# An attention kernel's setup in another order: Wk's transposes, sums and loads, Wq's spreading, and one batch's first head sums

## The chip, the cores and the metric

The kernel runs on one core of a Trainium2 chip. The metric is the device time of one execution in microseconds (us). A core has the engines PE (TensorE, matrix products; its weight loads are shown apart as PEld), DVE (VectorE), ACT (ScalarE), POOL (GpSimd) and SP (SyncE, which issues most of the DMAs). Each works through a list of instructions of its own, in order, and they wait for each other by semaphores.

## The reference

There are 16 batches with 100 query rows of width 640, and for each batch 722 context rows of width 384, of which the last 4 are "ca" tokens. There are 8 heads of 80 columns. Everything is in float32.

```python
query = hidden_states @ Wq
keyt, valt = enc @ Wk, enc @ Wv              # enc: the first 718 context rows
hs = _mha(query, keyt, valt)
ca_q1 = jnp.einsum('btc,th->bch', ca, Wq_ca)[:, indices, :]   # 100 picked columns
ca_hs1 = _mha(ca_q1, residual, residual)
ca_q2 = ca_hs1 @ Wq
ca_hs2 = _mha(ca_q2, ca @ Wk_ca, ca @ Wv_ca)
out = (hs + ca_hs2) @ Wout + b_out + residual
```

`_mha` is plain attention with a softmax over the keys of each head. `hs` is the large part, `ca_hs2` a small one with 4 keys.

## The kernel before, in words

**Stages.** A setup loads the weights and makes what the batches share; then a loop over 16 batches runs, in which scores, softmax, keys and values of the next batch, and the output projection are interleaved. Products of matrices are made by a scheme with fewer products and more sums (15 "forms" of sums of blocks), so the weights and the encoder rows are first added up: `weight_sums` (L546) for Wv, Wk and Wk's last part, `enc_sums` (L516) on POOL for each batch's encoder rows. A form's product goes to one of five banks of PSUM (A to E), and is copied (ACT, L423) or added (DVE, L421) into `kT` or `vs`.

**The setup around the change**, in the order of the text:

- SP's loads (from L287): encoder rows of batch 0, the ca tokens, Wk_ca, Wq transposed (L310), more encoder rows, x of batches 0 and 1 (`xT`, L313), `ca` of batch 0 (L315), then Wk transposed by `load_packed` (L317), Wq in five chunks of 128 rows (L323), Wv_ca (L324). Wk goes to the place of `kT`, Wq to the place of `sts`. `load_packed` turns the 640 rows (8 heads of 80) into five chunks of 128 rows: chunk c in 0 to 3 holds the first 64 rows of heads c and c + 4, chunk 4 the last 16 rows of all eight heads.
- PE makes values of batch 0 (L391), then `k_ps` (L1367) and the five m products (L1391); DVE copies each to `m_sb` (L1399), SP stores each to `m_d` (L1403).
- `y` (L970, in `Second.products`) multiplies x with `m2`, which POOL masks (`keys`, L941). DVE takes a part of y as `g` (`take`, L983), ACT copies the rest (L987).
- Wk's five chunks are transposed on PE (`w_ps`, L1415, chunk 4 first) and copied by ACT (L1418) to `wk4` and `wk_sb`.
- Wq's five chunks are spread by DVE into the order of heads that the products need, three copies each (L1426, L1432).
- DVE makes the 12 sums of Wk's blocks (L546), then takes the last head of `g` (L983). With that POOL makes the first scores of batch 0 (`scores1`, L999 and L1006), then 12 small sums of `wk4`.
- PE makes the last chunk of batch 0's keys (`last_keys`, `kT_ps`, L702), the keys by forms (`k_psA` and so on, L481), `va` (L1457) between them, and then the queries (`q_ps`, L560).
- SP loads the encoder rows of batch 1 (L234), its `ca` (L960) and the next `xT` (L218). `ca` has one buffer, so its load waits until POOL has read the one before.

**What sets the order.** In the setup the tile framework's scheduler decides: it orders each engine's instructions by its own model and by the order of the text, except where `in_order`/`keep_in_program_order` holds an instruction in its place, or `tc.issue_after(x)` puts the block behind x. From `tc.manual_schedule` on, the loop over the batches is in the order of the text.

**DMA issue.** The loads of SP and ACT use eight semaphores in turn, so a load is issued only when the eighth load before it has landed.

**Batch 14** (b = 14, `B - 2`): after its products with the values (`a_ps`, L1799), `read(g)` takes the reciprocal of the sums (L1747) and for each of four heads multiplies and adds `hs2` in one DVE instruction (L1759). In this batch `read(0)` stands in the middle of the second half, next to the search for the largest score of batch 15 (L891 to L926 and L918 on ACT), whose subtraction (L1025) and exponential (L1033) follow. The transposition of `hs` (L1197) and the output sums (`xn`, L1152 on POOL, L1339 on DVE) come later.

Of the kernel before, what the change touches and what calls it, by code (L numbers as in the profile page):

```python
# [10 lines left out]
ALU = mybir.AluOpType  # L11
# [3 lines left out]
B, S, H = 16, 100, 640  # L15
NH, D = 8, 80
CAD, T = 384, 4
SK = 722 - T
P = 128
HC = H // P  # L20
# [8 lines left out]
ROWS = NH * S  # L29
# [26 lines left out]
for h in range(NH):  # L56
    lo = h * D
    while lo < (h + 1) * D:
        c = lo // P
# [8 lines left out]
RG = 4  # L68
# [5 lines left out]
def load_packed(load, to, w):  # L74

    rows = w.rearrange("(h k) n -> h k n", h=NH)
    for h in range(NH):
        r, c = divmod(h, RG)
        load(out=to[64 * r : 64 * r + 64, c], in_=rows[h, :64])
    load(out=to[:, 4], in_=rows[:, 64:])  # L80


# [60 lines left out]
def kernel(  # L143
# [18 lines left out]
    nc = tc.nc  # L162
# [35 lines left out]
    def wide(name):  # L198
        return main.tile([P, ROWS], F32, tag="wide", name=name, bufs=2)

    sts = [main.tile([P, 2, ROWS], F32, name=f"st_{i}") for i in range(NP)]
# [58 lines left out]
    def in_order(dma):  # L260
        tc.keep_in_program_order(dma)
# [5 lines left out]
    wk_sb = const.tile([P, NF, 2, P], F32, name="wk_sb")  # L267
# [12 lines left out]
    enc = enc_tile("enc_0"), rest_tile("rest_0")  # L280
# [13 lines left out]
    for g in range(2):  # L294
        for c in range(CC):
            nc.scalar.dma_start(
                out=wv_sb[:, 2 * c + g],
                in_=wv[c * P : (c + 1) * P, g * (H // 2) : (g + 1) * (H // 2)],
# [13 lines left out]
    xT = inp.tile([P, 2, HC, S], F32, tag="xT", name="xT_0")  # L312
    in_order(nc.sync.dma_start(out=xT, in_=xt[0:2].rearrange("b p c s -> p b c s")))  # L313
    ca_0 = small.tile([S, T, S], F32, tag="ca", name="ca_0")
# [26 lines left out]
    for h, c, r, s, k in PIECES:  # L341
        nc.gpsimd.dma_start(
            out=m2[s : s + k, c, h - HEADS[c][0], :T],
# [153 lines left out]
    def enc_sums(enc):  # L497

        at = lambda f: a_form(enc, f)
        raw = lambda u, c: a_raw(enc, u - 1, c - 1)  # L500
        for out, left, right, op in (
            (at(7), raw(2, 3), raw(3, 1), ALU.add),
            (at(11), raw(3, 2), raw(3, 3), ALU.add),
            (at(8), at(11), raw(2, 3), ALU.subtract),
            (at(10), raw(1, 3), at(11), ALU.subtract),
            (at(9), raw(2, 1), raw(2, 2), ALU.add),
            (at(2), raw(1, 1), at(9), ALU.subtract),
            (at(9), at(9), raw(3, 1), ALU.subtract),
            (at(5), raw(1, 1), raw(2, 1), ALU.subtract),
            (at(5), at(5), raw(2, 3), ALU.add),  # L510
            (at(11), raw(1, 3), raw(3, 3), ALU.subtract),
            (at(11), at(11), raw(3, 1), ALU.add),
            (at(4), at(2), at(10), ALU.add),
            (at(4), at(4), raw(1, 2), ALU.add),
        ):
            nc.gpsimd.tensor_tensor(out, left, right, op)  # L516
# [7 lines left out]
    def weight_sums(engine, w, late=None, there={}):  # L524


        at = lambda f: there.get(f, w[:, W_AT[f]])
        raw = lambda c, g: w[:, 2 * (c - 1) + g - 1]
        if w is wk4:
            at, raw = w4_form, w4  # L530
        for f, left, right in (
            (0, raw(1, 2), raw(1, 1)),
            (11, raw(2, 2), raw(3, 2)),
            (12, raw(3, 2), raw(3, 1)),
            (5, raw(2, 2), raw(1, 2)),
            (7, raw(3, 2), at(5)),
            (13, raw(3, 1), at(7)),
            (1, raw(2, 1), raw(3, 1)),
            (3, raw(1, 1), at(7)),
            (6, raw(2, 1), raw(1, 1)),  # L540
            (10, raw(3, 1), raw(2, 2)),
            (2, raw(1, 1), raw(2, 2)),
            (14, raw(2, 1), raw(2, 2)),
        ):
            if late is None or late == (f in (5, 7, 13, 3, 14)):
                made = engine.tensor_tensor(at(f), left, right, ALU.subtract)  # L546
        return made
# [380 lines left out]
    def load_m(b):  # L928
        if b < 2:
            return lambda c: m_sb[c][:, b * HT : (b + 1) * HT]  # L930
        mb = small.tile([P, HC, HT], F32, tag="mb", name=f"mb_{b}", bufs=2)
        nc.sync.dma_start(
            out=mb, in_=m_d[:, :, b * HT : (b + 1) * HT].rearrange("c p n -> p c n")
        )
        return lambda c: mb[:, c]

    def keys(m):

        for c, heads in enumerate(HEADS):
            n = len(heads)  # L940
            made = nc.gpsimd.tensor_tensor(  # L941
                m2[:, c, :n, T:],
                m(c).unsqueeze(1).to_broadcast([P, n, HT]),
                hmask[:, c, :n].unsqueeze(2).to_broadcast([P, n, HT]),
                ALU.mult,
            )
        return made

    class Second:
# [35 lines left out]
        def copy(self):  # L985
            self.y = y_sbs[self.b % 2]
            nc.scalar.copy(self.y[:, :, :HT], self.y_v[:, :, T:])  # L987
            if self.b > 1:
                self.take(0, NH)
# [66 lines left out]
        def load(self, engine=nc.sync, behind=None):  # L1056
            self.vb = [self.piece(engine, t, behind) for t in range(2)]
# [318 lines left out]
    for n, heads in enumerate(HEADS):  # L1376
        cols = len(heads) * B * T
# [10 lines left out]
    for c in range(HC):  # L1388
# [12 lines left out]
            m_ps.rearrange("p (h b t) -> p h b t", h=NH, b=B),  # L1401
        )
        nc.sync.dma_start(out=m_d[c], in_=m_sb[c])  # L1403
    second = Second(0, xT, ca_0)
    enc_sums(enc)
    masked = keys(load_m(0))
    second.products()
    summed = second.take(0, NH - 1)
    second.copy()

    order = (HC - 1, *range(HC - 1))
    for c in order:
        w_ps = psum(f"w_ps_{c}")
        for cc in range(CC):
            nc.tensor.transpose(  # L1415
                w_ps[:, cc * P : (cc + 1) * P], wkt_sb[:, c, cc * P : (cc + 1) * P], ident
            )
        act(  # L1418
            wk_sb[:, c % 2 : 6 : 2, c // 2] if c < HC - 1 else wk4,
            w_ps[:, : CC * P].rearrange("p (a n) -> p a n", a=CC),  # L1420
        )

    with tc.issue_after(summed.ins):
        for c in range(HC):
            for r in range(2):
                nc.vector.tensor_copy(  # L1426
                    wq_sb[:, c, : 4 * P].rearrange("p (n r k) -> p n r k", n=RG, r=2)[
                        :, :, r
                    ],
                    wq_in[c].rearrange("p (r n k) -> p r n k", r=2, n=RG)[:, r, :, :64],  # L1430
                )
            moved = nc.vector.tensor_copy(  # L1432
                wq_sb[:, c, 4 * P :].rearrange("p (h k) -> p h k", h=NH),
                wq_in[c].rearrange("p (h k) -> p h k", h=NH)[:, :, 64:],
            )
    with tc.issue_after(moved.ins):
        made = weight_sums(nc.vector, wk_sb)
    with tc.issue_after(made.ins):
        second.take(NH - 1, NH)
    made = second.scores1()  # L1440
    with tc.issue_after(made.ins):
        weight_sums(nc.gpsimd, wk4)
        nc.scalar.copy(
            sts[0].rearrange("p a r -> p (a r)")[96:],
            low[96:].to_broadcast([P - 96, 2 * ROWS]),
        )
    with tc.issue_after(masked.ins):
        keys(load_m(1))
    last_keys(0, enc)
    first_keys = Keys(0, enc)  # L1450
    first_keys.go(8)
    va = wide("va")[:, : H // 2]
    va_ps = bank("va_ps")
    turn[0] += 1
    for c in range(CC):
        for n in range(2):
            nc.tensor.matmul(  # L1457
                va_ps[n * B * T : (n + 1) * B * T, : H // 2],
                cat_sb[:, c, :],
                wvca_sb[:, c, n * (H // 2) : (n + 1) * (H // 2)],  # L1460
                start=(c == 0),
                stop=(c == CC - 1),
            )
    nc.scalar.copy(va, va_ps[:, : H // 2])
    va_d = dram.tile([B * T, H], F32, name="va_d")
    for n in range(2):
# [2 lines left out]
            in_=va[n * B * T : (n + 1) * B * T],  # L1469
        )  # L1470
    first_keys.go(NF)
    with tc.issue_after(first_keys.added.ins):
        second.softmax1()

# [18 lines left out]
    for b in range(B):  # L1493
# [249 lines left out]
        def read(g):  # L1743

            a_v = a_vs[g]
            rs = small.tile([S, 4], F32, tag="rs", name=f"rs_{b}_{g}")
            nc.vector.reciprocal(rs.unsqueeze(2), a_v[:, :, D : D + 1])  # L1747
            cols = slice(4 * g * D, 4 * (g + 1) * D)
            if b == 0:
                nc.vector.tensor_tensor(  # L1750
                    hs[:S, cols].rearrange("p (h d) -> p h d", h=4),
                    a_v[:, :, :D],
                    rs.unsqueeze(2).to_broadcast([S, 4, D]),
                    ALU.mult,
                )
                return
            for h in range(4):
                part = slice((4 * g + h) * D, (4 * g + h + 1) * D)
                nc.vector.scalar_tensor_tensor(  # L1759
                    hs[:S, part],  # L1760
                    a_v[:, h, :D],
                    rs[:, h : h + 1],
                    hs2[:, part],
                    ALU.mult,
                    ALU.add,
                )

        if b in MIXED:
            steps = (0, 6), (0, 18), (1, 6)
# [112 lines left out]
```

## Time and profile before

| what | us |
|---|---|
| median of three runs (lowest, highest) | 907.91 (907.47, 909.91) |
| the profiled execution, as the device timed it | 908.96 |
| its span in the trace | 907.2 |
| PE busy | 900.4 |
| DVE, POOL, ACT busy | 719.7, 705.8, 460.1 |
| setup until the first query product | 50.0 |

The profile shows one execution. A row of the timeline gives the start and the length in us, the engine, the line of the kernel, the operation, the tiles and the count, and in brackets how long the engine stood idle before and what ended that. Rows of equal work that follow each other are merged, so a row's length spans them all. In a row of waits stand the total, the count and the longest. In a row of stretches (from:to) stand the length, the busy time of PE, PEld, DVE, ACT and POOL with their counts, the granted clock of PE (1.00 throughout), the busy share of the 16 DMA engines, and GB/s. The chain of waits follows the end of the run back, step by step, to what released each step.

### The profile page before, as it was taken

The numbers are of one execution on the slowest core, as the hardware profiler recorded it, in microseconds if no ns is written. First come the engines' busy times: TensorE is split into PE (matmuls) and PEld (weight loads), VectorE is DVE, ScalarE is ACT, GpSimd is POOL, SyncE is SP. The second block draws the span as 40 slices with busy tenths as digits, with TensorE's granted clock in tenths as the row PEclk, the third lists the DMA queues.
The fourth block names the chain that finished last, engine by engine and source line by source line (L and its number), as shares of the span: only waits on it lengthen the run. The fifth ranks groups of instructions, "written<-read, shape, count | busy, mean of one in ns | idle before, by whom it ended". The sixth has DMA issues, their size and how long they took to land.

```text
span 907.2 us, 28486 instructions
## 1 busy us (share of the span) xinstructions
PE 900.4 (99%) x12200; PEld 747.1 (82%) x12200; DVE 719.7 (79%) x1285; ACT 460.1 (51%) x906; POOL 705.8 (78%) x683
## 2 busy tenths in 40 slices
PE   9999999999999999999999999999999999999998
PEld 6798889787797878878798787988879788797866
DVE  3569796989849898796987969888984899849983
ACT  2345543747437573644737446374742747436441
POOL 7687999797868879696896959958797688967623
PEclk9999999999999999999999999999999999999999
DMA  8731103031301312130121301103130031300211
GB/s 265 262 120 57 48 14 87 24 107 53 112 4 44 88 33 74 54 105 32 48 60 54 106 33 53 56 25 106 54 83 32 24 107 53 98 32 25 60 44 40
DMA packets 50730, 62.99 MB, mean 69 GB/s; under 512 B 13698, under 2 KB 37954, under 8 KB 50604
## 3 DMA queue, kind: packets, MB, share of 16 engines
q1 hardware_dynamic: 48956, 59.18, 21.4%
q8 instruction: 96, 1.57, 0.7%
q10 hardware_dynamic: 1024, 1.15, 0.4%
q0 software_dynamic: 624, 0.85, 0.3%
q14 instruction: 30, 0.25, 0.1%
HBM read 55.59 MB, written 5.57 MB: 67 GB/s over the span
## 4 chain that ended last, share of the span: by engine, by line
PE 92%; DVE 4%; DMA 2%; SPq 1%; issue 0%; ACTq 0%; DVEq 0%
PE a_ps L1799 12%; PE s_ps L800 11%; PE v_psA L450 10%; PE k_psA L481 9%; PE v_psB L450 8%; PE k_psB L481 7%; PE o_ps L1278 5%; PE k_psA L761 4%; PE v_psC L450 3%; PE k_psC L481 3%; PE q_ps L618 2%; PE q_ps L560 2%; PE v_psD L450 2%; PE v_psE L450 2%; PE q_psA L618 1%; DMA xT<-in_xt 1%
## 5 line engine op out<-in xcount | busy, mean ns | idle before, releaser
L999 POOL TENSOR_TENSOR e<-ca,g 100x800 f32<-100x800 f32 x64 | 100.7, 1584 | 98.6 <-ACT kT L423 78.7
L1799 PEld LDWEIGHTS a_ps<-vs,st 120*64 120x64 f32 (+3 forms) x3072 | 119.0, 124 | 10.1 <-issue 0.7
L1799 PE MATMUL a_ps<-vs,st 120*64 120x81 f32 (+3 forms) x3072 | 122.8, 233 | 0.0
L516 POOL TENSOR_TENSOR enc<-enc 128x240 f32<-128x240 f32 x144 | 109.1, 768 | 11.3 <-DMA enc<-in_enct 4.2
L1515 DVE TENSOR_TENSOR st<-st,over 120x1600 f32<-120x1600 f32 x48 | 115.1, 2400 | 0.0
L450 PE MATMUL v_psA<-wv_sb,enc 128*120 128x320 f32 x352 | 109.3, 433 | 0.0
L1110 POOL TENSOR_TENSOR hs<-vb,p 100x640 f32<-100x640 f32 x64 | 93.1, 1466 | 9.6 <-issue 4.8
L1117 POOL TENSOR_TENSOR hs<-hs,hs 100x640 f32<-100x640 f32 x48 | 93.2, 1942 | 3.8
L481 PE MATMUL k_psA<-enc,wk_sb 128*128 128x240 f32 x384 | 95.4, 371 | 0.6 <-DVE wk_sb L546 0.6
L1006 POOL TENSOR_TENSOR e<-e,e 100x800 f32<-100x800 f32 x48 | 91.9, 1914 | 3.8
L450 PE MATMUL v_psB<-wv_sb,enc 128*120 128x320 f32 x296 | 91.9, 433 | 0.0
L1523 ACT ACTIVATE st<-st 120x1600 f32<-120x1600 f32 x48 | 73.9, 1539 | 25.1 <-DVE st L1515 24.7
L481 PEld LDWEIGHTS k_psA<-enc,wk_sb 128*128 128x128 f32 x384 | 71.4, 190 | 17.1 <-DVE wk_sb L546 1.0
L450 PEld LDWEIGHTS v_psA<-wv_sb,enc 128*120 128x120 f32 x352 | 64.2, 183 | 25.0 <-DVE vs L421 0.5
L1527 DVE TENSOR_TENSOR most<-most,st 120x800 f32<-120x800 f32 x64 | 67.0, 1047 | 13.8 <-ACT st L850 12.3
L481 PE MATMUL k_psB<-enc,wk_sb 128*128 128x240 f32 x320 | 77.9, 366 | 0.0
L800 PE MATMUL s_ps<-qp,kT 64*56 64x100 f32 (+1 forms) x3072 | 73.7, 248 | 0.3 <-issue 0.3
L800 PEld LDWEIGHTS s_ps<-qp,kT 64*56 64x56 f32 (+1 forms) x3072 | 67.2, 130 | 5.9 <-issue 4.6
L450 PEld LDWEIGHTS v_psB<-wv_sb,enc 128*120 128x120 f32 x296 | 54.1, 183 | 21.9 <-DVE vs L421 0.4
L856 ACT COPY st<-s_ps 120x800 f32<-120x800 f32 x64 | 49.8, 830 | 39.6 <-PE s_ps L800 39.4
L1185 ACT COPY hsT<-turned_hs 32x160 f32<-32x160 f32 (+7 forms) x244 | 67.7, 278 | 3.0
L481 PEld LDWEIGHTS k_psB<-enc,wk_sb 128*128 128x128 f32 x320 | 60.7, 190 | 8.1
(209 smaller groups left out, 1898.3 us busy)
## 6 DMA issues: line engine op xcount, KB each, us to landing
vb<-va_d SPq DMA_DIRECT2D x62, 250.0 KB
enc<-in_enct SPq DMA_DIRECT2D x30, 240.0 KB
enc<-in_enct SPq DMA_DIRECT2D x15, 360.0 KB
xT<-in_xt SPq DMA_DIRECT2D x8, 500.0 KB
rest<-in_enct SPq DMA_DIRECT2D x31, 120.0 KB
xn<-in_x SPq DMA_DIRECT2D x11, 320.0 KB
out<-xn SPq DMA_DIRECT2D x11, 320.0 KB
ca<-in_cas SPq DMA_DIRECT2D x16, 156.2 KB
```

Of the source, the lines that this page charges most:

```text
L450: nc.tensor.matmul(at[0][j][:KN, : H // 2], a_form(self.enc, f)[:, j * KN : (j + 1) * KN], wv_there.get(f, wv_sb[:, W_AT[f]]), start=first ...
L481: nc.tensor.matmul(at[:, i * KT : (i + 1) * KT], wk_sb[:, W_AT[f], i], a_form(self.enc, f), start=(first and i == 0), stop=last, skip_grou ...
L516: nc.gpsimd.tensor_tensor(out, left, right, op)
L800: nc.tensor.matmul(s_ps[at][k0:k1, cols], w, rhs, start=not begun & {(at, k) for k in range(k0, k1, 32)}, stop=last, skip_group_check=True,)
L999: first = nc.gpsimd.tensor_tensor(to, self.ca[:, t, :].unsqueeze(1).to_broadcast([S, NH, S]), g[:, :, t].unsqueeze(2).to_broadcast([S, NH, ...
L1006: made = nc.gpsimd.tensor_tensor(e, e, to, ALU.add)
L1110: first = nc.gpsimd.tensor_tensor(to, self.vb[t][:S].rearrange("p (h d) -> p h d", h=NH), p2[:, :, t].unsqueeze(2).to_broadcast([S, NH, D] ...
L1117: nc.gpsimd.tensor_tensor(sums, sums, to, ALU.add)
L1185: nc.scalar.copy(self.hsT(r)[32 * m : 32 * m + 32, :, first - lo : end - lo], turned[32 * i : 32 * i + 32, :, m, first - at : end - at],)
L1515: return nc.vector.tensor_tensor(st[i], st[i], top.over[:KN].unsqueeze(1).to_broadcast([KN, 2, ROWS]), ALU.subtract,)
L1523: nc.scalar.activation(st[i], st[i], AF.Exp, scale=SCALE)
L1799: nc.tensor.matmul(a_v[lo:hi, h % 4], st[i // 2][: KEYS[i], i % 2, h * S + lo : h * S + hi], block(i, h // 4)[: KEYS[i], h % 4], start=(i ...
```

## The change

1. Wk is loaded by five DMAs instead of nine: chunks 0 to 3 in one DMA each, over both heads (source: 2 blocks of 64 rows), chunk 4 as before (8 blocks of 16 rows).
2. The transposes of Wk and their copies stand ahead of `Second` in the text, and Wk's sums on DVE right behind them; PE then makes all 15 transposes before y.
3. Wq's spreading comes behind Wk's sums, chunks 0 to 2 on DVE, chunks 3 and 4 on ACT behind the first eight key forms.
4. The fill of `sts[0]`'s spare rows on ACT moves behind the keys; the first va product is held in its place.
5. In batch 14 the first half's four head sums become four products on ACT and one sum of 320 columns on POOL.

Built, the instructions stand so: PE has, after the m products, 15 transposes, y, `kT_ps`, and then the keys in the order A, B, D (D, A, B before). DVE has the 12 sums directly behind the m copies and `qmask`, then the first take of g, nine spreading copies, the second take. ACT has six spreading copies between the first three key copies and va's copy, and the fill behind the last key copy of batch 0. SP has batch 1's `ca` and the next `xT` ahead of batch 1's three encoder loads, which stood in front of them. POOL has the new sum ahead of the `xn` sums. From batch 0's scores to batch 14 nothing is changed on any engine.

```diff
 def load_packed(load, to, w):
     rows = w.rearrange("(h k) n -> h k n", h=NH)
-    for h in range(NH):
-        r, c = divmod(h, RG)
-        load(out=to[64 * r : 64 * r + 64, c], in_=rows[h, :64])
+    for c in range(RG):
+        load(out=to[:, c], in_=rows[c::RG, :64])
     load(out=to[:, 4], in_=rows[:, 64:])
...
-    second = Second(0, xT, ca_0)
-    enc_sums(enc)
-    masked = keys(load_m(0))
-    second.products()
-    summed = second.take(0, NH - 1)
-    second.copy()
-
     order = (HC - 1, *range(HC - 1))
     for c in order:
         w_ps = psum(f"w_ps_{c}")
...
-    with tc.issue_after(summed.ins):
-        for c in range(HC):
+    made = weight_sums(nc.vector, wk_sb)
+    second = Second(0, xT, ca_0)
+    enc_sums(enc)
+    masked = keys(load_m(0))
+    second.products()
+    second.take(0, NH - 1)
+    second.copy()
+
+    def spread_wq(copy, chunks):
+
+        for c in chunks:
             for r in range(2):
-                nc.vector.tensor_copy(
+                copy(
...
-            moved = nc.vector.tensor_copy(
+            moved = copy(
...
+        return moved
+
+    with tc.issue_after(made.ins):
+        moved = spread_wq(dve, range(3))
     with tc.issue_after(moved.ins):
-        made = weight_sums(nc.vector, wk_sb)
-    with tc.issue_after(made.ins):
         second.take(NH - 1, NH)
     made = second.scores1()
     with tc.issue_after(made.ins):
         weight_sums(nc.gpsimd, wk4)
-        nc.scalar.copy(
-            sts[0].rearrange("p a r -> p (a r)")[96:],
-            low[96:].to_broadcast([P - 96, 2 * ROWS]),
-        )
...
     first_keys.go(8)
+    spread_wq(lambda *ends: tc.keep_in_program_order(act(*ends)), range(3, HC))
...
-            nc.tensor.matmul(
+            made = nc.tensor.matmul(
                 va_ps[n * B * T : (n + 1) * B * T, : H // 2],
...
+            if c == n == 0:
+                in_order(made)
...
     first_keys.go(NF)
+    in_order(
+        nc.scalar.copy(
+            sts[0].rearrange("p a r -> p (a r)")[96:],
+            low[96:].to_broadcast([P - 96, 2 * ROWS]),
+        )
+    )
...
+                if b == B - 2 and g == 0:
+                    nc.scalar.mul(hs[:S, part], a_v[:, h, :D], rs[:, h : h + 1])
+                    continue
                 nc.vector.scalar_tensor_tensor(
...
+            if b == B - 2 and g == 0:
+                nc.gpsimd.tensor_tensor(hs[:S, cols], hs[:S, cols], hs2[:, cols], ALU.add)
```

## The prediction

> **What bounds the kernel now.** I read the page first, then the waits of PE (TensorE) by its weight loads (PEld), then the timeline and the chain of waits over the first 100 us, where all but one edit lies.
>
> ```profile
> span 907.2 us, 28486 instructions
> PE 900.4 (99%) x12200; PEld 747.1 (82%) x12200; DVE 719.7 (79%) x1285; ACT 460.1 (51%) x906; POOL 705.8 (78%) x683
> PE 92%; DVE 4%; DMA 2%; SPq 1%; issue 0%; ACTq 0%; DVEq 0%
> ```
>
> PE is busy for 99% of the span and is 92% of the chain that ended last. What other engines save is worth nothing, except where PE waits for it; and a new wait of PE comes off nothing else, it is added to the end. So I look for PE's waits, old and new.
>
> ```profile
> PEld w_ps L1415 <- DVE qmask L1476: 0.8, 1, 0.8
> PEld k_psA L481 <- DVE wk_sb L546: 1.0, 1, 1.0
> PEld w_ps L1415 <- ACT wk_sb L1418: 0.3, 1, 0.3
> ```
>
> These are the setup's waits in the whole run: about 2.1 us of weight-load time, before Wk's transposes and before the first key product. More the setup can't return. Now the stretch itself; the last two rows are from the chain.
>
> ```profile
> 27.31 0.83 PE L970 MATMUL y_ps<-m,xT 128*64 128x72 f32 x16
> 28.76 0.52 PE L1415 MATMUL w_ps<-ident,kT 128*128 128x128 f32 x3 [0.62 <-DMA kT<-in_wkt]
> 29.48 0.97 PEld L1415 LDWEIGHTS w_ps<-ident,kT 128*128 128x128 f32 x9
> 30.41 0.30 PEld L702 LDWEIGHTS kT_ps<-enc,wk 128*128 128x128 f32 x2
> ...
> 36.28 1.08 PE k_psA L481 x4
> ...
> 50.03 8.46 PE q_ps L560 x50
> 85.73 3.65 PE kT_ps L702 x18
> 96.29 0.75 PE y_ps L970 x20
> ```
>
> From the end of the m products (27.31) to the first query product (50.03) go 22.72 us. Pure work in it: 15 transposes at 0.103 (nine from 29.48 to 30.41) are 1.55; y 0.75; kT_ps 3.65; keys with va 13.75, plus 0.81 for the pair of D in front of them, less 0.27 (the first piece took 1.08 where others take 0.81): 14.29. With 0.15 for y, which has to wait for the third copy of a transpose, 20.4 us.
>
> **The new order.** After the m products PE does all 15 transposes, then y, then kT_ps, then the keys. If Wk is there at 27.31, q_ps begins at 27.31 + 20.4 = 47.7, 2.3 us earlier. In the old order y's first 16 products filled part of the wait for Wk; now y stands behind the transposes on PE, and the first transposes are those of chunk 4, whose load is issued last. So all hangs on when the fifth load lands.
>
> **Wk in five loads.** In bytes it is the same. But a load is not always spread over all 16 DMA engines, as these rows show (DMA share and GB/s are the last columns; in the SP rows L317 is Wk, L1062 va).
>
> ```profile
> 13.00:16.00 3.00, 3.00 (x13) 2.05 (x12) 0.00 (x0) 0.85 (x2) 2.77 (x6) 1.00 1.03 410
> 18.00:20.00 2.00, 2.00 (x38) 1.67 (x35) 0.91 (x4) 0.00 (x0) 0.00 (x0) 1.00 1.03 315
> 20.00:21.00 1.00, 1.00 (x6) 0.75 (x5) 0.31 (x2) 0.18 (x1) 0.98 (x2) 1.00 0.69 132
> 26.10:26.90 0.80, 0.80 (x8) 0.80 (x7) 0.69 (x1) 0.00 (x0) 0.78 (x4) 1.00 0.66 164
> 167.20:168.00 0.80, 0.80 (x5) 0.54 (x4) 0.74 (x4) 0.00 (x0) 0.72 (x2) 1.00 0.66 262
> ...
> 19.90 1.74 SPq L317 DMA_DIRECT2D kT<-in_wkt  x3
> ...
> 23.70 1.32 SPq L317 DMA_DIRECT2D kT<-in_wkt  x2
> ...
> 164.64 0.71 SPq L1062 DMA_DIRECT2D vb<-va_d  x2
> ```
>
> Loads of 128 rows fill all 16: share 1.03, 410 GB/s, 25.6 GB/s an engine. At 167.2 two loads of 100 rows are under way together, and still only 0.66 of the engines work, at 262 GB/s: ten engines (16 would give 410), and the same ten for both, or the two would have covered more. At 26.1 the old ninth Wk load runs nearly alone; its source is 8 blocks of 16 rows, and the rate is 164 GB/s, under half. Sixteen for 128, ten for 100, half or fewer for 8 blocks: the engines go by the count of the outermost dimension, and loads that get fewer share the same ones. The new loads `rows[c::RG, :64]` have 2 blocks of 64 rows: I take two engines, the same two for the four loads. [...]
>
> One of the four loads is 192 KB (196,608 bytes), 98,304 bytes for each of the two engines: 3.84 us at 25.6 GB/s; 4.80 at 164 / 8 = 20.5 GB/s, the rate of the ninth load with its start in it. I take 4.2, nearer to the dense rows. The queue ahead (share 1.03 up to 20, 0.69 after) is through at about 20.5; the first three loads are issued by then and the rest follow at once, so nothing but the two engines paces them. 20.5 + 4 x 4.2 = 37.3. The fifth load (8 blocks) has 24,576 bytes on each of eight engines, behind the others on the two: 1.05, so 38.35, and PE begins its transposes at 38.45, 11.1 us after the m products. 38.45 + 20.4 = 58.85 for q_ps, against 50.03: **+8.8 us**. Bounds: drained at 20 and 3.84 a load gives 36.4, so +6.8; drained at 21 and 4.80 gives 41.5, so +11.9.
>
> **What else moves**, at that time:
>
> ```profile
> 29.71 0.48 DVE L1426 COPY wq_sb<-st 128x256 f32<-128x256 f32 x2
> 30.09 1.27 ACT L1418 COPY wk_sb<-w_ps 128x384 f32<-128x384 f32 x3
> 33.46 4.11 DVE L546 TENSOR_TENSOR wk_sb<-wk_sb 128x256 f32<-128x256 f32 x12
> 37.71 3.04 POOL L999 TENSOR_TENSOR e<-ca,g 100x800 f32<-100x800 f32 x2 [6.70 <-DVE g L983]
> ...
> 44.13 0.43 ACT L1464 COPY va<-va_ps 128x320 f32<-128x320 f32 x1 [5.37 <-PE va_ps L1457]
> ...
> 47.93 0.32 SPq L960 DMA_DIRECT2D ca<-in_cas  x1
> ...
> 53.16 0.69 POOL L516 TENSOR_TENSOR enc<-enc 128x240 f32<-128x240 f32 x1
> 56.13 1.30 DVE L1025 TENSOR_TENSOR e<-e,over 100x800 f32<-100x800 f32 x1
> 60.92 2.14 POOL L516 TENSOR_TENSOR enc<-enc 128x240 f32<-128x240 f32 x3
> 62.37 0.88 ACT L1033 ACTIVATE e<-e 100x800 f32<-100x800 f32 x1
> ...
> 66.86 1.08 PE L481 MATMUL k_psA<-enc,wk_sb 128*128 128x240 f32 x4
> ```
>
> - Wk's sums: ScalarE's five copies of the transposes end near 41.2 (0.42 each), the sums 12 x 0.343 later at 45.2; the first eight, after which k_psA went before, at 43.9. PE comes to k_psA at 44.55. Hidden, with 0.6 to spare.
> - Wq's chunks 0 to 2 on DVE (0.48 for two of the three copies, about 0.7 in all), then the last head of g: POOL's score products start at 47.5 instead of 37.71, 9.8 later against PE's 8.8. What they lead to was ready at 57.43 (L1025) for an exponential at 62.37; the 1.0 is hidden.
> - Chunks 3 and 4 on ScalarE: no row has such a copy; between half and all of the 0.42 that 384 columns take, 6 of them 1.3 to 2.5, in ScalarE's idle 5.37 before va. Nothing. The 1.5 us fill of st, now ahead of the queries' copies, ends long before the first scores.
> - Wq, wvca and the m stores queue behind Wk on the two engines, at 0.8 us per Wq load and 2.5 for wvca: 42.5 and 45. The sums hold DVE until 45.2, and va comes 6 us into the keys, at 51. Hidden.
> - On SP the loads of batch 1's enc now stand behind its ca, which waits for POOL's last score product (47.93 before, 57.7 now). They land near 63, POOL's 9.9 us of sums (53.16 to 63.06) end near 73; they ended at 63.06 before a product at 66.86, which is now at 75.7. Hidden, with 2.5 us.
>
> **Batch 14.**
>
> ```profile
> 849.80 3.30 POOL L1152 TENSOR_TENSOR xn<-xn,bias 128x640 f32<-128x640 f32 x3
> 855.68 0.93 DVE L1759 SCALAR_TENSOR_TENSOR hs_sb<-a_ps,rs,hs 100x80 f32<-100x80 f32 x4
> 857.19 1.73 ACT L918 COPY spread<-mx 64x800 f32<-64x800 f32 x2 [0.83 <-DVE mx L905]
> 860.00 0.99 DVE L1025 TENSOR_TENSOR e<-e,over 100x800 f32<-100x800 f32 x1
> 861.19 1.68 ACT L850 COPY st<-s_ps 120x400 f32<-120x400 f32 x4 [0.31 <-PE s_ps L800]
> 862.74 1.00 ACT L1033 ACTIVATE e<-e 100x400 f32<-100x400 f32 x2
> 871.71 0.49 DVE L1339 TENSOR_TENSOR xn<-o_ps,xn 128x320 f32<-128x320 f32 x1 [0.27 <-issue]
> ```
>
> DVE loses 0.93 us, ScalarE gains four products ahead of the spread, whose price no row has: from DVE's own 0.23 each to twice that. The spread moves by between 0 and +0.9. The subtraction that follows ended at 860.99; its exponential came at 862.74, behind the copies of L850, so 1.7 us are covered, and an earlier subtraction wins nothing. POOL's added sum, after the products, holds the xn sums (four, some 5 us) till about 858; they end at 863 and are needed at 871.71. Zero, both ways.
>
> **The sum.** The profiled execution took 908.96 for a span of 907.2. By this its changed twin has 917.8; on the median of 907.91 the forecast is 916.7 us, with the bounds 914.7 and 919.8.
>
> **Rivals.**
> 1. The new loads use all 16 engines. Wk then lands about 25.5, before 27.31, and q_ps moves to 47.7: 907.91 - 2.3 = 905.6, not slower. For it: 128 destination rows, and 410 GB/s for such loads. Against: the ninth load has 128 destination rows too and ran at 164. It decides at 27.31 + 2.3 = 29.6: Wk landing before that is a gain, later a loss. Chance 0.09.
> 2. Two engines each, but another pair for each load. Four loads side by side end at 21 + 4.2, and it is 905.6 again. Against: the two vb loads kept to one set of ten. Chance 0.05.
> 3. Two engines, and each slower than 20.5 GB/s, for rows that come from memory one at a time: half the rate, 10.2, would put Wk at 61 and the time near 940. Against: 26 GB/s an engine in the vb row, also with fewer than 16. Chance 0.03.
>
> **Chances.** Forecast 0.83. The range 914.0 to 920.0 holds it nearly whole, and leaves out the rest, 0.17. A difference under 0.3% (2.7 us) is about what a measurement of this kernel can't tell from none; rivals 1 and 2 (2.3) lie in it. Slower by over 0.3%: 0.86; within: 0.13; faster, which would need more than all of the setup's waits: 0.01.
>
> **What would show it.** Right: PE idle for some 11 us before w_ps, ended by the DMA of kT; a DMA share near 0.13 (2 of 16) and some 50 GB/s between 28 and 36; the waits for Wk's sums gone from PE's list; nothing new from batch 0's scores on. Wrong: transposes at 27.3 with no wait. If the wait is there but far from 11 us, the rate of one engine was wrong; if a second wait of PE follows it, one of the covers above.

## The result, and the profile after

The changed kernel takes **923.33 us** (median of 6 runs, 922.43 to 924.76) against 907.86 for the kernel before (6 runs beside it, 907.47 to 909.91): ratio 1.0168, 95% interval 1.0155 to 1.0181, 15.5 us slower. The forecast was 916.7, with a range of 914.0 to 920.0. The sign and the mechanism were right; the size, 8.8 us, was little more than half of what came. The profiled execution took 923.1 us for a span of 921.4, which is 14.2 more than the span of before; the kernel before was profiled in an execution 1.1 us above its median of 907.86.

The head of the page, as it was read of before:

```profile
span 921.4 us, 28485 instructions
PE 902.8 (98%) x12200; PEld 749.5 (81%) x12200; DVE 723.1 (78%) x1275; ACT 462.8 (50%) x916; POOL 709.5 (77%) x684
PEclk9799999999999999999999999999999999999999
PE 93%; DMA 3%; DVE 2%; SPq 1%; ACT 0%; issue 0%; ACTq 0%; DVEq 0%
```

PE is the bound as before. New is a 7 in the row of the granted TensorE clock, in the second slice of 23 us. In the chain the DMA's share rose from 2% to 3% and DVE's fell from 4% to 2%. The waits of PE, and one of its weight loads:

```profile
PE w_ps L1407 <- DMA kT<-in_wkt: 12.2, 1, 12.2
PE k_psA L480 <- DVE kT L420: 1.4, 1, 1.4
PE k_psB L480 <- DVE sm L1091: 0.3, 1, 0.3
PEld k_psA L480 <- POOL e L998: 1.9, 1, 1.9
```

The first row is the wait that was forecast (11 us). The wait for Wk's sums (`wk_sb`) is gone. The other three rows, all in batch 0, were not forecast: the prediction said "if a second wait of PE follows it, one of the covers above" had failed. The chain of waits (start, length, what), cut to the places that matter:

```profile
20.93 3.82 SPq L316
24.80 14.92 DMA kT<-in_wkt
39.85 3.43 PE w_ps L1407 x15
43.28 1.63 PE y_ps L969 x19
...
62.94 8.46 PE q_ps L559 x50
...
82.08 3.97 DVE most L1534
...
104.71 1.32 PE a_ps L1811 x32
```

The transposes start at 39.85, 1.4 later than forecast, and take 3.43 us for 15, where 1.55 had been reckoned. The first query product starts at 62.94 (50.03 before, +12.9; forecast +8.8). The head sums of batch 0 (`a_ps`) start at 104.71 (89.38 in the chain of before, +15.3), so 2.4 us more were lost between the two. After that the distance stays at 15.3 up to batch 10.

Windows of the changed kernel (from:to, length, busy time of PE, PEld, DVE, ACT and POOL; then the granted clock, the DMA share and GB/s):

```profile
22.00:24.00 2.00, 2.00 (x17) 2.00 (x17) 0.96 (x2) 0.00 (x0) 1.92 (x4) 1.00 0.14 53
26.00:28.00 2.00, 1.66 (x13) 1.47 (x11) 1.00 (x2) 0.00 (x0) 0.70 (x3) 1.00 0.13 50
30.00:32.00 2.00, 0.00 (x0) 0.00 (x0) 0.00 (x0) 0.00 (x0) 0.00 (x0) 0.84 0.96 273
34.00:36.00 2.00, 0.00 (x0) 0.00 (x0) 0.00 (x0) 0.00 (x0) 0.00 (x0) 0.50 1.00 291
42.00:44.00 2.00, 2.00 (x19) 1.67 (x19) 0.81 (x3) 1.44 (x3) 0.00 (x0) 0.50 0.81 292
```

Three things are to be seen. From 22 to 28 the DMA share is 0.13, two engines of 16, at 50 GB/s: the two engines of the forecast. From 30 on the share is 1.0, but at 290 GB/s, where loads of 128 rows had moved 410 before: the other fourteen engines move Wq and wvca beside them (SP issued Wq from 28.66, wvca at 32.98). And the clock falls to 0.50 in the wait and is still there when PE works again at 42 to 44.

### The profile page after: what moved, and what is told of

It reads as the page before. It is cut to its first block, busy times and chain, and to the rows that moved or that the text cites. A ratio compares the mean times of both kernels' runs of the same rounds, so it can differ in the third digit from the quotient of the medians.

```text
span 921.4 us, 28485 instructions
## 1 busy us (share of the span) xinstructions
PE 902.8 (98%) x12200; PEld 749.5 (81%) x12200; DVE 723.1 (78%) x1275; ACT 462.8 (50%) x916; POOL 709.5 (77%) x684
## 4 chain that ended last, share of the span: by engine, by line
PE 93%; DMA 3%; DVE 2%; SPq 1%; ACT 0%; issue 0%; ACTq 0%; DVEq 0%
PE a_ps L1811 12%; PE s_ps L799 11%; PE v_psA L449 11%; PE v_psB L449 9%; PE k_psA L480 8%; PE k_psB L480 7%; PE o_ps L1277 5%; PE k_psA L760 4%; PE v_psC L449 4%; PE k_psC L480 3%; PE q_ps L617 2%; PE q_ps L559 2%; PE v_psD L449 2%; PE v_psE L449 2%; DMA kT<-in_wkt 2%; PE q_psA L617 1%
## 5 line engine op out<-in xcount | busy, mean ns | idle before, releaser
L998 POOL TENSOR_TENSOR e<-ca,g 100x800 f32<-100x800 f32 x64 | 99.5, 1566 | 91.1 <-ACT kT L422 78.5
L515 POOL TENSOR_TENSOR enc<-enc 128x240 f32<-128x240 f32 x144 | 110.1, 775 | 14.3 <-DMA enc<-in_enct 7.3
L1116 POOL TENSOR_TENSOR hs<-hs,hs 100x640 f32<-100x640 f32 x48 | 97.0, 2020 | 3.8
L1109 POOL TENSOR_TENSOR hs<-vb,p 100x640 f32<-100x640 f32 x64 | 89.1, 1402 | 9.1 <-issue 4.8
L1534 DVE TENSOR_TENSOR most<-most,st 120x800 f32<-120x800 f32 x64 | 69.1, 1080 | 13.5 <-ACT st L849 12.3
```

The costliest lines, as they stand in the source:

```text
L998: first = nc.gpsimd.tensor_tensor(to, self.ca[:, t, :].unsqueeze(1).to_broadcast([S, NH, S]), g[:, :, t].unsqueeze(2).to_broadcast([S, NH, ...
L1109: first = nc.gpsimd.tensor_tensor(to, self.vb[t][:S].rearrange("p (h d) -> p h d", h=NH), p2[:, :, t].unsqueeze(2).to_broadcast([S, NH, D] ...
L1116: nc.gpsimd.tensor_tensor(sums, sums, to, ALU.add)
L1534: most_now = nc.vector.tensor_tensor(most[:KN], most[:KN], st[i][:, u], ALU.max)
```

## The experiments

Theory A, from this profile: (1) the five loads alone cost the time, through two engines; (2) PE runs at half clock for some us after the wait; (3) batch 1's enc loads, behind `ca` on SP, make POOL late, and this costs 2.4 us in batch 0. Rivals: the new order costs by itself (B), few and large loads are slow (C), the maxima on DVE are slow anyway (D), ScalarE's copies pace the transposes (E).

### Nine loads, with all the rest of the change

```diff
-    for c in range(RG):
-        load(out=to[:, c], in_=rows[c::RG, :64])
+    for h in range(NH):
+        r, c = divmod(h, RG)
+        load(out=to[64 * r : 64 * r + 64, c], in_=rows[h, :64])
```

> The changed kernel with Wk's nine loads of before (64 rows each, and the last of 8 blocks of 16); the new order and batch 14's edit stay. Theory A (the loads alone cost the time: two DMA engines, the half clock after the wait, and batch 1's enc loads behind ca): Wk is in at about 28.6 as before, so PE waits some 1.3 us for it, the granted clock stays at 1.0, the first query product starts at about 49.2 (50.03 before, 62.94 changed), and batch 0 has no waits of PE for DVE. Time 906 to 907.5, against 907.86 before. Theory B (the new order costs by itself, with y, the sums and the spreading of Wq pushed back): the first query product comes after 50 and PE still waits for DVE in batch 0, time 909 or more.

Measured: 908.61 us against 908.84 for the kernel before on this chip, ratio 1.0001, 0.9993 to 1.0010 (11 and 23 runs). The first query product starts at 49.70, 0.3 us earlier than before. So the whole loss goes with the loads, and B falls in its main point. But the 906 to 907.5 of A were too low: the new order wins 0.3 us until there, not 0.8, and that can't be told from nothing.

### Three loads, 64 rows outermost

```diff
-    for c in range(RG):
-        load(out=to[:, c], in_=rows[c::RG, :64])
+    for r in range(2):
+        load(
+            out=to[64 * r : 64 * r + 64, :RG],
+            in_=rows[RG * r : RG * r + RG, :64].rearrange("h k n -> k h n"),
+        )
```

> The changed kernel with Wk in three loads: two of four heads each, with the 64 rows as the outermost dimension on both sides (64 rows x 4 heads x 384), and the last as it is. Theory A (the count of the outermost dimension sets the engines): 16 engines, Wk in between 25 and 28, PE waits under 0.8 us for it, the first query product between 47.7 and 48.5, time 905 to 906.5. Rival C (few and large loads are slow, because many small ones overlap better or one load holds the queue): three loads are at least as late as five, Wk in at 38 or later, and a time of 920 or more.

Measured: 908.18 us, ratio 1.0001, 0.9990 to 1.0012. From its windows and its chain:

```profile
22.00:24.00 2.00, 2.00 (x18) 2.00 (x17) 1.27 (x2) 0.00 (x0) 1.92 (x4) 1.00 1.09 214
```

```profile
28.50 1.83 PE w_ps L1410 x15
30.40 1.10 PE y_ps L972 x20
...
49.51 8.46 PE q_ps L562 x50
```

Fewer loads than five, and 15 us faster: C falls. With 64 rows outermost the share is 1.09, all 16 engines, where 2 blocks had 0.13; but they move only 214 GB/s. The 905 to 906.5 of A were too low here as well. Wk is in just before 28.50, not much earlier than with nine loads, and this is why nothing is won over the kernel before. The chain also gives the prediction's "pure work" at full clock without the wait: 49.51 - 28.50 = 21.0, where 20.4 had been reckoned (transposes 1.83 and y 1.10 with the gaps around them, not 1.55 and 0.75).

### The five loads alone, in the kernel before

The edit is the first one in the other direction: the five loads put into the kernel before, nothing else.

> The kernel before with the five loads alone; old order, no edit of batch 14. Theory A: Wk in at about 39.7 as in the changed kernel, the wait of PE 12 us or more, the transposes at half clock (0.21 us each instead of 0.10); the sums wait on DVE behind the whole spreading of Wq, which lands last at 45.5, so the first key product waits about 1 us more; the first query product near 63, batch 1's enc behind ca on SP here too, time 921 to 924.5. Theory B (half of the loss is the new order): time under 919.

Measured: 922.54 us (920.65 to 923.41, 4 runs), ratio 1.0151, 1.0138 to 1.0164. The old order with the five loads loses 13.7 us, nearly all of the change's loss, and its interval meets the changed kernel's (1.0155 to 1.0181). Its chain has the transposes from 40.54, the first query product at 62.34 and the head sums of batch 0 at 101.69, 12.3 later than before. So the loss up to the queries is here, and the 2.4 us behind them are not.

### Batch 1's enc ahead of its ca

```diff
+    moved_enc = [None]
...
-            nc.sync.dma_start(
+            moved_enc[0] = nc.sync.dma_start(
...
-    last, enc_next, second_next = None, load_rest(1, load_enc(1)), Second(1, xT)
+    last, enc_next = None, load_rest(1, load_enc(1))
+    with tc.issue_after(moved_enc[0].ins):
+        second_next = Second(1, xT)
```

> The changed kernel with the loads of batch 1's enc ahead of its ca on SP; nothing else. Theory A: enc is issued when the products of va end (57), 3.6 us earlier; POOL's sums start at about 65.3 instead of 68.87 and end near 77.4, before the products of ca and g; the waits of PE for DVE in batch 0 (1.4, 0.6 and 0.3 us) go, and the time falls by 1.5 to 2.5 us to 921 to 922. Rival D (the waits come from DVE and POOL meeting in the maxima whatever POOL's start): the time stays within 0.5 us of 923.3 and the maxima still take 4 to 5 us for two.

Measured: 921.14 us (920.5 to 922.4, 4 runs), 2.2 under the changed kernel; ratio to the kernel before 1.0140, 1.0127 to 1.0153, under the changed kernel's interval. From the first query product to batch 0's head sums are 39.4 us, as before (41.8 in the changed kernel), and the waits of PE for DVE in batch 0 are gone. The profiled execution, the slowest of the four, has a span only 0.7 shorter than the changed kernel's: its first query product is 0.45 later and 0.6 are lost again in batch 1. First the rows of the changed kernel, from the timelines of SP, POOL and DVE (L959 is `ca`, L233 enc, L515 the sums, L998 the products of ca and g, L1534 the maxima):

```profile
59.99 0.31 SPq L959 DMA_DIRECT2D ca<-in_cas  x1
60.77 2.02 SPq L233 DMA_DIRECT2D enc<-in_enct  x3
68.87 0.69 POOL L515 TENSOR_TENSOR enc<-enc 128x240 f32<-128x240 f32 x1 [3.60 <-DMA enc<-in_enct]
82.14 3.04 POOL L998 TENSOR_TENSOR e<-ca,g 100x800 f32<-100x800 f32 x2
81.06 4.97 DVE L1534 TENSOR_TENSOR most<-most,st 120x800 f32<-120x800 f32 x2
```

Then the same two groups with enc first:

```profile
80.87 3.23 DVE L1538 TENSOR_TENSOR most<-most,st 120x800 f32<-120x800 f32 x2
81.09 4.41 POOL L1000 TENSOR_TENSOR e<-ca,g 100x800 f32<-100x800 f32 x2 [4.25 <-ACT st L857]
```

And with the five loads alone, where enc stands behind `ca` too:

```profile
80.16 2.38 DVE L1526 TENSOR_TENSOR most<-most,st 120x800 f32<-120x800 f32 x2
82.80 3.04 POOL L998 TENSOR_TENSOR e<-ca,g 100x800 f32<-100x800 f32 x2
```

In the kernel before:

```profile
67.46 3.23 DVE L1527 TENSOR_TENSOR most<-most,st 120x800 f32<-120x800 f32 x2
67.68 4.41 POOL L999 TENSOR_TENSOR e<-ca,g 100x800 f32<-100x800 f32 x2 [3.54 <-ACT st L856]
```

Where POOL is ready and starts 0.2 us after DVE's pair, as before the change and with enc first, POOL pays most: 4.41 for its two instead of 3.04, and the pair takes 3.23 instead of 2.38. Where POOL comes 1.1 us later, its two products fall on DVE's second maximum, and DVE pays: 4.97. Where it comes after the pair has ended, nobody pays (2.38 and 3.04). Of what follows the maxima on DVE, the key form's addition (`kT`) is what PE waits for. So A's third part is shown, and D falls: the 2.4 us come from when POOL starts. In the changed kernel DVE's second maximum started at 82.08, POOL's first product at 82.14. The maximum, though it started first, took 3.97 us, to 0.9 after the end of both products, and these took no longer than behind the pair (3.04).

### TensorE kept at work in the wait

```diff
+    for half in range(2):
+        warm_ps = psum(f"warm_{half}")
+        for _ in range(27):
+            in_order(
+                nc.tensor.matmul(
+                    warm_ps[:, :P], idle, idle, start=True, stop=True
+                )
+            )
...
```

`idle` is a tile of zeros. The transposes behind the products are held in their place too.

> The changed kernel with 54 products of a zero tile (128x128, results unused, some 11.5 us) between the m products and Wk's transposes, so that TensorE is at work in its wait for Wk. Theory A (the granted clock falls to half after some 3.5 us of idling, which costs 2.1 us after the wait): the granted clock stays at 1.0, the 15 transposes take 1.8 instead of 3.43 us, y 1.1 instead of 1.63, and the first query product starts about 2.1 us earlier, at 60.9; time 920.5 to 921.5, or 919 if batch 0's waits for DVE go with it. Rival E (the transposes are slow because ScalarE's copies of 0.48 us pace them): 3.4 us again, and the time stays at 923.

Measured: 920.52 us (919.51 to 921.25, 4 runs), 2.8 under the changed kernel; ratio 1.0132, 1.0119 to 1.0145. Its chain, and one window:

```profile
27.50 12.06 PE warm L1407 x108
39.56 1.73 PE w_ps L1416 x15
41.36 1.13 PE y_ps L969 x20
60.44 8.46 PE q_ps L559 x50
```

```profile
42.00:44.00 2.00, 2.00 (x21) 1.82 (x17) 2.00 (x6) 0.03 (x1) 1.81 (x5) 1.00 0.83 283
```

54 products whose results nobody reads (108 in the trace's count) make the kernel faster. The clock stays at 1.00, the transposes take 1.73, and 39.56 to 60.44 are 20.9 us where the changed kernel takes 23.1 for the same work (39.85 to 62.94). E falls. In this profile POOL was also in time (pair 3.23), which wins 2.4 more until batch 1; 1.3 of these 4.9 us is lost again later, 0.8 of it in batch 1. So the 919 that had been expected for this case did not come.

With enc first in addition:

> The changed kernel with the 54 products in the wait for Wk and with batch 1's enc ahead of its ca. Theory A: what is left is the wait for Wk itself, 10.9 to 12 us later than before less the 2.3 that the new order wins, and 0.6 of work that was taken too short: first query product at 60.5, time 918.5 to 920.5. The run with the products alone showed no meeting of POOL and DVE either (the pair took 3.23), so nothing much is won over its 920.5.

Measured: 920.39 us (919.62 to 920.5, 4 runs), first query product at 61.47, a microsecond later than expected (Wk came 0.9 us after the last of the products). The time is the same as with the products alone, as expected.

### Two of the four loads

```diff
-    for c in range(RG):
+    for c in range(2):
         load(out=to[:, c], in_=rows[c::RG, :64])
+    for h in (2, 3, 6, 7):
+        r, c = divmod(h, RG)
+        load(out=to[64 * r : 64 * r + 64, c], in_=rows[h, :64])
```

> The changed kernel with only two of the four loads of 2 blocks (heads 0 and 4, 1 and 5); the other four heads by 64 rows each, and the last load as it is. Theory A (two engines, 4.1 us for each such load, one behind the other): these two are through at about 28.2, the four others and the last one have their share on the same two engines behind them, so that Wk is in at 30.3 to 31.6; PE waits 3 to 4.3 us, the first query product starts between 51.3 and 53.5, and the time is 909.5 to 913, or up to 915.5 with the waits of batch 0. Rival C (the size or number of loads sets it, or each pair of blocks finds engines of its own): no wait of PE over 1.5 us, time under 909.2.

Measured: 913.65 us (913.35 to 913.91, 4 runs), ratio 1.0057, 1.0044 to 1.0070. The wait is 5.0 us, the transposes start at 32.30, 0.7 later than the upper end, and take 3.44 us, at half clock again; the first query product starts at 55.23. Two such loads fewer bring Wk 7.55 us earlier (39.85 to 32.30), 3.8 for each: they stand one behind the other, as A says, and C falls here too. The time and the first query product are above the ranges that were expected (913 and 53.5; the rest up to 915.5 was kept for waits in batch 0, which did not come): the half clock behind the wait was not reckoned in full.

### Wq and wvca ahead of Wk

The edit moves the six loads of Wq and wvca on SP in front of Wk's five.

> The changed kernel with the loads of Wq and wvca ahead of Wk's five. In the changed kernel the four two-engine loads took 4.1, 4.1, 4.6 and 5.4 us, the last two while the other fourteen engines moved Wq (300 GB/s in all). Theory A (the traffic of the others slows the two engines): with Wq and wvca gone first (2.6 MB, 6.5 us from 20.2), the two engines run alone for the whole stretch, DMA share 0.13 and 50 GB/s, 4.1 us for each, and Wk is in at 43.6 to 44.6; the time is 927 to 930. Rival K (loads that queue for longer get slower by themselves, 19.5 us for the five whenever they run): Wk in at 46 or later.

Measured: 925.22 us (2 runs), ratio 1.0183, 1.0165 to 1.0201. PE's timeline shows when the chunks land, since here it takes them as they come:

```profile
31.43 0.52 PE L1407 MATMUL w_ps<-ident,kT 128*128 128x128 f32 x3 [4.23 <-DMA kT<-in_wkt]
39.28 0.87 PE L1407 MATMUL w_ps<-ident,kT 128*128 128x128 f32 x3 [7.33 <-DMA kT<-in_wkt]
44.23 2.37 PE L1407 MATMUL w_ps<-ident,kT 128*128 128x128 f32 x9 [4.08 <-DMA kT<-in_wkt]
```

```profile
28.00:30.00 2.00, 0.00 (x0) 0.00 (x0) 0.13 (x1) 0.00 (x0) 0.29 (x1) 1.00 0.13 49
34.00:36.00 2.00, 0.00 (x0) 0.00 (x0) 0.00 (x0) 0.00 (x0) 0.00 (x0) 0.50 0.13 50
38.00:40.00 2.00, 0.72 (x3) 0.50 (x3) 0.00 (x0) 0.00 (x0) 0.00 (x0) 0.50 1.05 403
```

First load 31.4, third 39.28: 3.9 each, and the landing events give 4.05 for the last of the four and 1.0 for the fifth. Wk is in at 44.2, inside A's range; K falls. In the changed kernel the landing events have 4.1, 4.1, 4.7 and 5.5, then 1.3. So the prediction's price of 4.2 was near for engines that run undisturbed, and with the loads of Wq and wvca beside them Wk's took 2.6 us more from the first landing to the last (15.5 against 12.9).

But it isn't traffic as such, as A had it: the two engines did not run alone to the end here. From 38 to 40 the others were busy too (share 1.05, 403 GB/s, mostly SP's stores of m, issued from 35.91), and the two loads of that time took 3.8 and 4.05. Nor were these stores the cause in the changed kernel: there SP issued them from 38.51 on, when the fourth load had landed. Why these loads slow Wk's, and stores of m don't, was not tried. The time is below what was expected (927 to 930): POOL was in time here, and six transposes were done in the wait.

### Batch 14 alone

The kernel before with only the last part of the change: four products on ScalarE and one sum on POOL in batch 14.

> The kernel before with batch 14's edit alone. The prediction on record: nothing, both ways. Theory A now: the changed kernel's offset falls by 0.5 us across batch 14, where the kernel before has a wait of 0.5 us before its score products that names no releaser; so 0.3 to 0.6 us earlier here too, 908.3 beside 908.8, hard to tell in the times but plain in the trace. Rival F (the offset fell for the different phase of the engines, not for the edit): the wait is still there and batch 14 ends at the same distance from batch 13 as before.

Measured: 908.98 us against 909.11, ratio 1.0003, 0.9995 to 1.0012. From the waits of PE's weight loads from 862 to 905, first the kernel before, then this one:

```profile
PEld v_psA L450 <- DVE vs L421: 0.5, 2, 0.3
PEld s_ps L800 <- issue: 0.5, 1, 0.5
```

```profile
PEld v_psA L450 <- DVE vs L421: 0.8, 2, 0.5
PEld v_psC L450 <- DVE vs L421: 0.5, 1, 0.5
```

The 0.5 without a releaser is gone and 0.8 of waits for DVE's `vs` have come. In the run of the five loads alone, without this edit, the 0.5 without a releaser is gone too. So the wait went, which F had not expected, but the kernel won nothing by it, as F said: A was wrong on the time, and the edit is worth nothing, as the prediction on record had it.

### Wk on two queues, then with enc first

```diff
...
-    for r in range(2):
-        load(
+    for r, queue in enumerate((load, other)):
+        queue(
             out=to[64 * r : 64 * r + 64, :RG],
             in_=rows[RG * r : RG * r + RG, :64].rearrange("h k n -> k h n"),
         )
```

> The changed kernel with Wk in three loads, 64 rows outermost, the first half (partitions 0 to 63) on SyncE's queue and the second (64 to 127) on ScalarE's. Theory G: in the run with three loads on one queue the 16 engines were all busy (share 1.09) but moved only 180 to 214 GB/s, half of the 410 of loads of 128 rows, because each load reaches half of the partitions; side by side the two halves move at about 400. Wk is in at 24 to 25.5, before the m products end, PE's wait before the transposes falls from 1.2 to 0.8 us or less (the last copy of m), the first query product starts at 48.4 to 49.1, time 0.5 to 1.2 us under the run with three loads. Rival H: the two share the same engines and take turns, so nothing is won: Wk in at 28 again, first query product at 49.5, the same time. [...]

Measured: 910.05 us against 909.11, ratio 1.0017, 1.0006 to 1.0028: a loss, though Wk was in before the m products ended and the first query product started at 48.60, 1.4 earlier than before. Wk was earlier because ScalarE issued its half at 6.2, where SyncE comes to its own at 14.2. By the DMA's packets in the trace ScalarE's half moved from 7.8 to 11.1 us and SyncE's loads from 20.3 on: the two halves never moved side by side, so neither G nor H was put to the test. The rate of SyncE's half from 22 to 24 was 199 GB/s at a share of 1.08, no better than with one queue. What ate the gain is in the timelines of DVE and POOL, and SP has `ca` ahead of enc again in this build:

```profile
67.01 4.96 DVE L1540 TENSOR_TENSOR most<-most,st 120x800 f32<-120x800 f32 x2
68.08 3.04 POOL L1004 TENSOR_TENSOR e<-ca,g 100x800 f32<-100x800 f32 x2
```

The meeting of the changed kernel without its loads. So enc was put first:

> The run on two queues, with the loads of batch 1's enc ahead of its ca on SyncE as well. There POOL started its products of ca and g 1.1 us after the second pair of DVE's maxima, and that pair took 4.96 us; in every run in which POOL was there first and started 0.2 us after the pair, it took 3.23 (and POOL's own pair 4.41 instead of 3.04). Theory A: POOL's sums end before DVE has g, the pairs take 3.23 and 4.41, the waits of PE for DVE in batch 0 (1.9 and 0.3 us) go, the 1.4 us won before the first query product stay won, and the time is 906.5 to 908 against 909.1 for the kernel before on this chip. Rival (the two queues cost elsewhere): 909 to 910 as before, with the pairs at 3.23.

```profile
65.67 3.23 DVE L1544 TENSOR_TENSOR most<-most,st 120x800 f32<-120x800 f32 x2
65.89 4.41 POOL L1006 TENSOR_TENSOR e<-ca,g 100x800 f32<-100x800 f32 x2 [3.63 <-ACT st L863]
```

Measured: 907.83 us against 908.74 (12 and 17 runs), 2.2 under the run before it; ratio to the kernel before 0.9996, 0.9985 to 1.0007 (1.0017 without enc first). The pair is at 3.23, the waits are gone and the first query product starts at 48.19. ScalarE's half of Wk, 64 rows to partitions 64 to 127, had the engines nearly to itself for a microsecond:

```profile
8.00:9.00 1.00, 1.00 (x5) 0.71 (x5) 1.00 (x3) 0.51 (x2) 0.86 (x3) 1.00 0.86 278
```

At 278 GB/s, a load to half of the partitions isn't held to the 199 and 214 of SyncE's by that alone, and G's reason falls. What slows SyncE's halves stays open. This run is the best version, 15 us under the changed kernel; over the kernel before no gain is shown.

## Why the prediction was wrong in size

**Point by point.**

- *PE is the bound, and what it waits for is added to the end*: right.
- *Two engines for a load of 2 blocks, the same two for all*: right (share 0.13, 50 GB/s; the runs with three, five and seven loads).
- *38.35 for the last load*, by 4.2 us a load: 39.7, inside the bounds of 36.4 and 41.5. Wrong was "nothing but the two engines paces them": beside the loads of Wq and wvca Wk's took 2.6 us more than with these out of the way, and the last two of the four fell to 21 and 18 GB/s an engine; without them the price was 4.05. The row from 26.1, read as eight engines by its rate, has a share of 0.66, which is more than eight: Wq's first load, issued at 25.07, was under way in it. So its 20.5 GB/s an engine, on which the upper bound rests, is no clean price of one load. Beside this, "the rest follow at once" did not hold: SP took 3.82 us to issue a load and the five took 16.28 us (13.04 for the nine), but the two engines had work all the time, so it cost nothing. +1.4.
- *20.4 us from the transposes to the first query product*: 21.0 at full clock (three loads). Transposes and y take 1.83 and 1.10 there, where rows of single pieces had given 1.55 and 0.75. +0.6.
- *The 20.4 us taken at the durations of before*: **the first failing step.** Durations of a PE that had never stopped were used behind a wait of 12 us. The granted clock fell to 0.50 at about 31.4, 3.7 us after PE stopped, and was full again at 45.0, 5.1 us after it restarted (the two windows below are of the changed kernel). +2.1, shown by the run with PE kept at work. The times differ from run to run: the clock fell 2.9 us after PE stopped with two such loads, 5.2 with the five loads alone, and was full 4.7 and 3.2 us after the restart. The prediction did not weigh it, and no row of before shows it: the clock is 1.00 throughout there, and no wait of PE is longer than 1.1 us.

```profile
31.00:31.50 0.50, 0.00 (x0) 0.00 (x0) 0.00 (x0) 0.00 (x0) 0.00 (x0) 0.86 0.95 199
45.00:45.50 0.50, 0.50 (x3) 0.47 (x4) 0.50 (x3) 0.00 (x0) 0.50 (x2) 0.99 0.43 148
```

- *Batch 1's enc behind ca, hidden with 2.5 us*: **the second failing step.** The order was seen, the price was not: enc was in 8.9 us after `ca` was issued (59.99 to 68.87), not 5.3, with the next `xT` between the two on the queue, and POOL's sums took 12.2 us, not 9.9, and ended at 81.0, not 73. And the check was made at the wrong place. PE's first key product, at 79.76, did not wait for the sums; what stood behind them on POOL, the products of ca and g, came 1.1 us after DVE's pair had begun and held up its second maximum. This is the second wait of PE that the prediction named as its sign of a failed cover. +2.4, shown by putting enc first.
- *Wk's sums, Wq's copies on DVE and ScalarE, the fill*: hidden, as said (six copies on ScalarE took 1.72 us; bounds 1.3 to 2.5).
- *Batch 14 zero*: right.
- *Rivals 1 to 3*: none came. Whether 16 engines would have brought rival 1's 905.6 isn't shown: no run has its loads. The nearest, the run with three, whose two large loads go to 64 partitions each, had Wk in just before 28.5, not at rival 1's 25.5, with 214 GB/s.

**The sum.** 8.8 + 1.4 + 0.6 + 2.1 = 12.9 at the first query product, as measured; + 2.4 = 15.3 at batch 0's head sums. Later 1.1 us come back: the kernel before has waits of 0.7 (`k_psC` for DVE) and 0.5 us there, the changed one other and shorter ones; this part was read from the two traces only and not tried. That leaves the 14.2 of the spans, and 15.5 between the medians for the reason given at the top. The late Wk alone, at +10.2, would have stayed inside the prediction's bounds of +6.8 and +11.9; the half clock and the second wait took the time out of the range.

**What stays open.** Why the loads of Wq and wvca slow the two engines of Wk's, and why batch 1 eats 0.6 to 0.8 us of what some versions win, was not tried.

## What to carry to other kernels

Before a DMA is made larger, look at the outermost dimension of its source too: 2 blocks of 64 rows, to 128 rows of the destination, meant two engines here (share 0.13), and the four loads queued on the same two. Where a change makes TensorE wait, look at the granted clock behind the wait: here, in waits of 5.0 and 12.2 us, it fell to 0.50 some 2.9 to 5.2 us after TensorE stopped, and was full 3.2 to 5.1 us after the restart. And where a cover is reckoned for an engine, follow it to the next instruction on that engine and ask whom that one will meet, not only who reads the covered result.

## What the runs showed of the hardware that was not expected

- SyncE's loads to 64 partitions filled all 16 engines (share 1.08 and 1.09) and moved 199 and 214 GB/s, where loads of 128 rows had moved 410; ScalarE's half of the same shape moved 278 GB/s at a share of 0.86. So a full share isn't the full rate.
- Loads on the other fourteen engines (Wq, wvca) slowed Wk's on the two, from 4.05 to 5.5 us for the fourth load; stores (of m), at 403 GB/s in all, did not.
- A short piece of work didn't keep the clock: with Wq first, three transposes (0.52 us) in a wait ended at 31.95, and the granted clock was 0.51 from 32.5 on.
- Issuing the loads that two engines moved was slow: SP needed 3.82 us to issue one load of 192 KB, and 16.28 for the five, where the nine took 13.04.
